# A state-space stage re-ordered by the size of the array pieces its matmuls use

## The chip, the cores and the metric

The kernel runs on one core of a Trainium2 chip, in one launch, all data in 32-bit floats. The metric is the device time of the launch in microseconds (us). Inside the core five engines run side by side, each with its own queue of instructions in a fixed order: TensorE (PE in the profile, its weight loads PEld), VectorE (DVE), ScalarE (ACT), GpSimd (POOL) and SyncE (SP), which issues most DMAs. TensorE writes only to PSUM; VectorE and ScalarE read the results from there.

## What is computed

Two layers on an image of 4 samples, 128 channels, 64 x 64 pixels. Layer 0 is three convolutions and an attention; layer 1 takes the pixels as 4 sequences of 4096 tokens through a state-space block run in both directions, and then through a recurrence. The change is in the state-space block:

```python
def _mamba3(x, in_proj, conv_w, conv_b, A_log, dt_bias, D, norm_w, out_proj):
    zxbcdt = x @ in_proj
    z, xbc, dt = jnp.split(zxbcdt, [D_INNER, D_INNER + CONV_DIM], axis=-1)
    xp = jnp.pad(xbc, ((0, 0), (K - 1, 0), (0, 0)))
    conv = sum((xp[:, i:i + l, :] * conv_w[:, i] for i in range(K))) + conv_b
    xh, Bm, Cm = jnp.split(_silu(conv), [D_INNER, D_INNER + D_STATE], axis=-1)
    dt = softplus(dt + dt_bias)
    A = -jnp.exp(A_log)
    y = _ssd(xh, dt, A, Bm, Cm) + xh * D[None, None, :, None]
    yg = y.reshape(b, l, D_INNER) * silu(z)
    yn = yg * rsqrt(jnp.mean(yg * yg, -1, keepdims=True) + EPS) * norm_w
    return yn @ out_proj

# _ssd, per chunk of tokens, per head (4 heads of 64 channels, 64 states):
Y_diag = einsum('bcln,bcsn,bchls,bcshp->bclhp', Cc, Bc, Lmat, xc)   # inside a chunk
states = einsum('bcln,bclh,bclhp->bchpn', Bc, decay_st, xc)         # what a chunk adds
new = st + carry * dec                                              # carried on
Y_off = einsum('bcln,bchpn,bclh->bclhp', Cc, prev, exp(Acs))        # from the carried state

t = t + _mamba3(ln(t), fwd...) + flip(_mamba3(flip(ln(t)), bwd...))
```


## The kernel before

The function `mamba` does both directions at once. Channels lie on the 128 partitions, tokens along the free axis. A **step** is a chunk of 128 tokens of each direction; a sequence has 32 steps and the four sequences follow one another, 128 steps in all. Four steps are a **group** of 512 tokens, 32 groups in all; j, from 0 to 3, is the place of a step in its group. Projections are made a group at a time, one group ahead.

The order on TensorE and ScalarE is that of the program text (`manual_schedule`, with these two engines); VectorE, GpSimd and SyncE get theirs from the scheduler of the framework. The loop over n (from line 1409 on) writes in each step:

- `states(m[n])`, L1212: what chunk n adds to the state, into `p_st`. Two matmuls with 64 output columns each, one for each direction: the two column halves of the array. VectorE adds it to the decayed state S (L1224).
- `turn(m[n+1])`, L1177: four 128 x 128 transposes of x of the next step into `ptr` (one buffer in PSUM). VectorE multiplies it by dt and by the decay into `xdt` and `xdtd` (L1196).
- `scan(m[n])`: eight matmuls `y<-lt,xdt` (L1234) in column halves, and then eight matmuls `y<-ct,S` (L1242) for the carried states, each with 64 rows and 64 columns, a quarter of the array.
- `prepare(m[n+1])`: the transpose of B into `p_bt` (L1187), two matmuls of B with C into `p_g` (L1189) with 64 rows and 128 columns each; then on ScalarE Exp of `lt` (L1191) and the copy `bt` (L1193); on VectorE xdt, xdtd, `gm` (L1200) and `lt` times gm (L1201); on GpSimd `ct` (L1202).
- `take`, for odd n: y plus D times x, on VectorE (L1254), which frees the PSUM tile y for the next two steps.
- projections by j. j = 0: px (L1124), pb for B (L1103), px. j = 1: pm, the means (L1283), px, pb for C. j = 2: px with four taps (L1115), four pz (L1146). j = 3: two po, the output (L1308).
- `differences(m[n+2])`: eight Relu on ScalarE (L1168) that prepare lt.
- on certain steps a part of a generator. `open_sequence(b+1)` prepares the next sequence: its first eight parts (steps 4 to 11 of a sequence) each transpose four tiles (`ls_in`, L83) for the row statistics, with bn_stats on VectorE (L85). `ended(b-1)` does the same for the sequence before, on odd steps from 5 on. For the last sequence `own` does it on steps 24, 25, 28 and 29.

All matmuls with px, pz and po use all 128 rows and 128 columns of the array (shown as `128*128`); pb uses column halves (`128*64`), the two directions being the halves. A 32-bit matmul runs as two rows in the profile, a transpose as one.

px, pb, pm, pz, po and ls_in take their PSUM from one pool, `ring`, with three buffers in turn: an allocation waits until the third one before it has been read out. Of px, ScalarE reads the first tap and VectorE three more (L1135, scalar_tensor_tensor), in place along x. `small` is one PSUM tile that holds `p_g`, `p_bt` and `p_st`.

Of the kernel before, what the change touches and what calls it, by code (L numbers as in the profile page):

```python
# [887 lines left out]
def mamba(nc, tc, k, a, t, B, T, vec, first=None, after=None, mr=None):  # L888
# [16 lines left out]
    with ExitStack() as ctx:  # L905
# [26 lines left out]
        bc_bias, dtb, A = vec["bc_bias"], vec["dtb"], vec["A"]  # L932
        wdt = wp.tile([P, QT], F32, name="wdt")
        nc.gpsimd.memset(wdt, 0.0)
        mean = wp.tile([P, QT], F32, name="mean")
        nc.gpsimd.memset(mean, 0.0)
        nc.gpsimd.memset(mean[:, 0:1], 1.0 / DI)
        with tc.tile_pool(name="m_ws", bufs=1) as ws, tc.tile_pool(name="m_wps", bufs=2, space=PSUM) as wps:
# [51 lines left out]
        ctx.enter_context(tc.manual_schedule(engines=set(engines)))  # L990
        small = ps.tile([P, 2, NC], F32, name="small")
        p_g, p_bt, p_st = small[:, :, 0:P], small[:, 0, P : 2 * P], small[:, 1, P : P + DI]

        def rows(g, i, c):

            return ds(g * MG + c if i == 0 else (NG - 1 - g) * MG + 2 * PAD - c, MG)
# [113 lines left out]
        def project_fwd(gr):  # L1110

            tl, g = gr["tl"], gr["at"][1]
            px = ring.tile([P, MG], F32, tag="big", name="px")
            for tap in range(KC):
                nc.tensor.matmul(px, w[0]["x"][:, tap, :], tl[:, rows(g, 0, tap)], start=(tap == 0), stop=(tap == KC - 1))  # L1115
            nc.scalar.activation(gr["x"][0][:, 0, :], px, AF.Silu, bias=w[0]["cb"][:, 0:1])

        def project(gr, i, c):


            tl, g = gr["tl"], gr["at"][1]
            px = ring.tile([P, MG], F32, tag="big", name="px")
            wx = w[1]["x"][:, bass.ts(c, P)] if i else w[0]["x1"]
            nc.tensor.matmul(px, wx, tl[:, rows(g, i, PAD)], start=True, stop=True)  # L1124
            x = gr["x+"][i][:, c, :]
            taps = w[i]["taps"][:, c, :]
            at = lambda n: x[:, PAD - n : PAD - n + MG] if i else x[:, n : n + MG]
            nc.vector.memset(x[:, 0:PAD] if i else x[:, MG:], 0.0)
            nc.scalar.activation(at(0), px, AF.Identity, scale=taps[:, PAD:KC], bias=w[i]["cb"][:, c : c + 1])  # L1129
            if g:  # L1130
                v = x[:, MG:] if i else x[:, 0:PAD]
                past = groups[gr["at"][0] * NG + g - 1]["x+"][i][:, c, :]
                nc.vector.tensor_tensor(v, v, past[:, 0:PAD] if i else past[:, MG:], ALU.add)
            for n in range(1, KC):
                nc.vector.scalar_tensor_tensor(at(n), px, taps[:, PAD - n : KC - n], at(n), ALU.mult, ALU.add)  # L1135
# [5 lines left out]
        def project_z(gr, i, c):  # L1141
            tl, g = gr["tl"], gr["at"][1]
            if c == 0:
                gr["z"][i] = grp.tile([P, 2, MG], F32, tag=f"z{i}", name=f"zT{i}", bufs=1)
            pz = ring.tile([P, MG], F32, tag="big", name="pz")
            nc.tensor.matmul(pz, w[i]["z"][:, bass.ts(c, P)], tl[:, rows(g, i, PAD)], start=True, stop=True)  # L1146
            nc.scalar.activation(gr["z"][i][:, c, :], pz, AF.Silu)

        def load(m):
# [20 lines left out]
        def turn(m):  # L1170

            gr, i = m["g"], m["i"]
            m["tok"] = [bass.ts(i % MT, P), bass.ts(MT - 1 - i % MT, P)]
            m["xh"] = ps.tile([P, ND, NHEAD, HD], F32, tag="tr", name="ptr")
            for d in range(ND):
                for c in range(2):
                    nc.tensor.transpose(  # L1177
                        m["xh"][:, d, 2 * c : 2 * c + 2, :].rearrange("p h c -> p (h c)"),
                        gr["x"][d][:, c, m["tok"][d]], k.ident,
                    )  # L1180

        def prepare(m):

            gr, i = m["g"], m["i"]
            Bs, Cs = gr["bc"][0], gr["bc"][1]
            cols = bass.ts(i % MT, P)
            nc.tensor.transpose(p_bt, Bs[:, cols], k.ident)  # L1187
            for d in range(ND):
                nc.tensor.matmul(p_g[:, d, :], Bs[HALF[d], cols], Cs[HALF[d], cols], start=True, stop=True)  # L1189
            lt = m["lt"]  # L1190
            nc.scalar.activation(lt, lt, AF.Exp, scale=-1.0)  # L1191
            m["bt"] = wk.tile([P, P], F32, tag="bt", name="bt")
            nc.scalar.copy(m["bt"], p_bt)  # L1193
            for name in ("dt", "dtd"):
                m[name] = wk.tile([P, ND, NHEAD, HD], F32, tag="x" + name, name="x" + name)
                nc.vector.tensor_tensor(  # L1196
                    m[name], m["xh"], m["b"][name][:, :, i, :].unsqueeze(3).to_broadcast([P, ND, NHEAD, HD]), ALU.mult
                )
            gm = wk.tile([P, ND, P], F32, tag="gm", name="gm")
            nc.vector.tensor_tensor(gm, p_g, k.tri, ALU.mult)  # L1200
            nc.vector.tensor_tensor(lt, lt, gm.unsqueeze(2).to_broadcast([P, ND, NHEAD, P]), ALU.mult)  # L1201
            nc.gpsimd.tensor_tensor(  # L1202
                m["ct"], m["ct"], Cs[:, cols].unsqueeze(1).to_broadcast([P, NHEAD, P]), ALU.mult
            )

        def states(m, S):
# [20 lines left out]
        def scan(m, y, S):  # L1227

            i = m["i"]
            at = [bass.ts(i % 2, P), bass.ts(1 - i % 2, P)]  # L1230
            for c in range(2):
                for d in range(ND):
                    for h in range(2):
                        nc.tensor.matmul(  # L1234
                            y[HALF[h], d, c, at[d]], m["dt"][:, d, 2 * c + h, :], m["lt"][:, d, 2 * c + h, :],
                            start=(i % 2 == 0 and c == 0), stop=(S is None), skip_group_check=True,
                        )
            if S is not None:
                for c in range(2):
                    for h in range(2):  # L1240
                        for d in range(ND):
                            nc.tensor.matmul(  # L1242
                                y[HALF[h], d, c, at[d]], S[HALF[d], 2 * c + h, :], m["ct"][HALF[d], 2 * c + h, :],
                                start=False, stop=True, skip_group_check=True,
                            )
# [13 lines left out]
        def half(d, i):  # L1259

            return bass.ts(i if d == 0 else 1 - i, 2 * P)
# [16 lines left out]
        def means(gr):  # L1278


            pm = ring.tile([ND * QT, MG], F32, tag="big", name="pm")
            for d in range(ND):
                nc.tensor.matmul(  # L1283
                    pm[bass.ts(d, QT)], mean, gr["z"][d][:, 0, :], start=True, stop=True, tile_position=(0, d * QT)
                )
            ms = wk.tile([ND * QT, MG], F32, tag="row", name="ms", bufs=3)
            nc.vector.tensor_scalar(ms, pm, RMS_EPS, None, ALU.add)
            n = ND * MG // P
            m1 = dram.tile([P, n], F32, tag="m1", name="m1")
            nc.sync.dma_start(m1.rearrange("(d q) n -> d (q n)", d=ND), ms[::QT])  # L1290
            col = wk.tile([P, n], F32, tag="col", name="col")
            nc.sync.dma_start(col, m1)
            rsqrt(nc, k, col, col)
# [10 lines left out]
        def outputs(gr, d):  # L1304
            po = ring.tile([P, MG], F32, tag="big", name="po")
            for i in range(2):
                for c in range(2):
                    nc.tensor.matmul(  # L1308
                        po[:, half(d, i)], w[d]["out"][:, c, :], gr["y"][d][i][:, c, :],
                        start=(c == 0), stop=(c == 1),  # L1310
                    )
            return po

        def means_here(gr):
# [88 lines left out]
        for i, c in STEPS_X:  # L1403
            activate(groups[0], i, c)
        turn(m[0])
        prepare(m[0])
        differences(m[1])
        S, y = None, None
        for n in range(N):
# [6 lines left out]
            if n % NT == 0:  # L1416
                S = None
            S1 = states(m[n], S)
            if n + 1 < N:
                turn(m[n + 1])  # L1420
            if n % 2 == 0:
                y = ps.tile([P, ND, 2, 2 * P], F32, tag="y", name="y")
            scan(m.pop(n), y, S)
            S = S1
            if n + 1 < N:
                prepare(m[n + 1])
            if n % 2:
                take(gr, j, y)
# [35 lines left out]
            if n + 2 < N:  # L1464
                differences(m[n + 2])

            i = n % NT
            if i == 4:
                opening = open_sequence(b + 1) if b + 1 < B else iter(())
            if i >= 4:  # L1470
                run(islice(opening, 1))
            if i == 5:
                ending = ended(b - 1) if after is not None and b > 0 else iter(())
            if i >= 5 and i % 2:
                run(islice(ending, 1))

            if mr is not None and b == B - 1 and i in (24, 25, 28, 29):
                if i == 24:
                    own = row_statistics(nc, k, ring, "big", wk, t[:, b * T :], mr, (3, 4, 2, 5, 1, 6))
                next(own)  # L1480
        squares(gr, (1,), True)
        if mr is not None:
            run(own)
# [273 lines left out]
```

## Time and profile before

| | |
|---|---|
| time, 3 runs | 3138.46, 3139.4, 3145.35 us; median 3139.4 |
| span of the profiled execution | 3147.0 us |
| state-space stage in it, first to last write of the states | 1718.7 to 2983.5 us |
| busy in that stretch (1264.8 us) | PE 1194.6, DVE 889.0, ACT 1014.1, POOL 725.0 us |
| mean granted TensorE clock in it | 0.98 |
| wait of PE at B's transpose for VectorE's S | 26 times, 26.4 us |

The profile is one execution. Its page has the busy time of each engine, the span in 40 slices, the chain of work that ended last, the costliest groups of instructions and the DMAs. Views of the trace answer for a stretch of time: the windows view gives the busy time of each engine in a stretch; the timeline gives instructions in order, each with start, duration, engine, line, operation, what it writes and reads, shape, count and, in brackets, the idle time before it and what ended it. Matmuls are pipelined and the end of each is modelled, so that neighbouring rows overlap: the step from one start to the next is what counts. The page puts the stage's lines low in its list because the attention before it has more instructions; the chain that ended last names PE first (26% of the span), with `pb L1103` as its costliest line (5%).

### The profile page before, as it was taken

What the parts mean: (1) busy time and instruction counts of PE and PEld (TensorE: products, weight loads), DVE (VectorE), ACT (ScalarE), POOL (GpSimd) and SP (SyncE); (2) the same over time, 40 slices, a digit from 0 to 9 for tenths busy, and PEclk for the clock granted to TensorE, in tenths of its full rate; (3) what the DMA queues carried; (4) which work ended last, traced back from release to release, by engine and by line L of the source; (5) the groups of instructions that cost most, each with busy time, mean ns of one, the idle gap of its engine ahead of it and who ended that gap; (6) DMA issues with size and microseconds to landing.
All of it is one profiled execution on the core that took longest, in us unless ns stands there. A gap on an engine that the chain in (4) does not pass through costs nothing. (4 is left out here: it accounts for less than half of the span.)

```text
span 3147.0 us, 42863 instructions
## 1 busy us (share of the span) xinstructions
PE 2925.4 (93%) x15511; PEld 1458.2 (46%) x15511; DVE 2195.2 (70%) x3429; ACT 1813.8 (58%) x3102; POOL 1798.5 (57%) x1393
## 2 busy tenths in 40 slices
PE   6799999999999999999997999999999999999976
PEld 1344444454444454444453444444444444455545
DVE  7876668666777667687765767776677766777667
ACT  3343434433444434444434878887788778888756
POOL 4258448456584665766553565565555565565644
PEclk9999999999999999999998999999999999999988
DMA  5310101010100101010023343334333343333332
GB/s 181 133 39 30 38 31 45 8 43 23 46 23 30 43 23 38 31 52 33 11 74 92 91 117 95 98 95 115 82 100 94 80 120 89 105 95 103 87 109 109
DMA packets 108394, 224.16 MB, mean 71 GB/s; under 512 B 25678, under 2 KB 29390, under 8 KB 106764
## 3 DMA queue, kind: packets, MB, share of 16 engines
q1 hardware_dynamic: 96588, 177.53, 19.9%
q10 hardware_dynamic: 11584, 43.78, 4.1%
q8 instruction: 125, 2.05, 0.3%
q14 instruction: 97, 0.79, 0.1%
HBM read 200.83 MB, written 20.44 MB: 70 GB/s over the span
## 5 line engine op out<-in xcount | busy, mean ns | idle before, releaser
L477 DVE TENSOR_TENSOR es<-es,ex 128x1024 f32<-128x1024 f32 x448 | 683.2, 1525 | 139.2 <-ACT ex L462 105.8
L462 ACT ACTIVATE ex<-pf 128x1024 f32<-128x1024 f32 x512 | 497.6, 1021 | 464.7 <-PE pf L460 421.2
L460 PE MATMUL pf<-theta,phi 64*128 64x512 f32 x2048 | 513.6, 619 | 20.4 <-ACT ex L462 20.0
L471 PE MATMUL acc<-ex,gT 128*64 128x512 f32 x2048 | 492.8, 607 | 1.7 <-ACT ex L462 1.7
L1202 POOL TENSOR_TENSOR ct<-ct,Cst 128x512 f32<-128x512 f32 x128 | 170.7, 1334 | 343.6 <-DMA ct<-csmem 314.1
L460 PEld LDWEIGHTS pf<-theta,phi 64*128 64x128 f32 x2048 | 173.0, 185 | 340.0 <-ACT ex L462 172.3
L1168 ACT ACTIVATE lt<-lt,cs 128x128 f32<-128x128 f32 x1024 | 312.1, 390 | 0.5 <-DMA lt<-csmem 0.5
L367 PE MATMUL pm<-yf,wt 128*128 128x256 f32 x1152 | 287.1, 382 | 11.9 <-DVE att L483 11.0
L410 ACT ACTIVATE eo<-pm 128x256 f32<-128x256 f32 x88 | 33.7, 383 | 448.9 <-PE pm L367 442.3
L471 PEld LDWEIGHTS acc<-ex,gT 128*64 128x64 f32 x2048 | 127.9, 137 | 339.8 <-issue 327.8
L367 PEld LDWEIGHTS pm<-yf,wt 128*128 128x128 f32 x1152 | 212.9, 189 | 93.4 <-issue 38.7
L1103 PE MATMUL pb<-tl,wbc_fwd 128*64 128x512 f32 x512 | 241.9, 616 | 6.5 <-DVE xT L1135 6.5
L1103 PE MATMUL pb<-tl,wbc_bwd 128*64 128x512 f32 x512 | 242.5, 617 | 0.0
L337 POOL TENSOR_TENSOR yf<-yd 128x272 f32<-128x272 f32 x192 | 234.0, 1246 | 1.4
L1267 POOL TENSOR_TENSOR yT<-yT,zT 128x512 f32<-128x512 f32 x127 | 166.5, 1316 | 58.1 <-DVE yT L1254 50.0
L337 POOL TENSOR_TENSOR yf<-xp 128x272 f32<-128x272 f32 x128 | 108.7, 880 | 136.0 <-PE pm L367 130.2
L1201 DVE TENSOR_TENSOR lt<-lt,gm 128x1024 f32<-128x1024 f32 x128 | 179.2, 1400 | 1.9
L1135 DVE SCALAR_TENSOR_TENSOR xT<-px,taps_bwd,xT 128x512 f32<-128x512 f32 x192 | 143.7, 748 | 8.7 <-ACT xT L1129 4.0
L1234 PE MATMUL y<-lt,xdt 128*64 128x128 f32 x2048 | 142.3, 282 | 7.6 <-PE ptr L1177 3.8
L1221 POOL TENSOR_TENSOR S<-S,tot 128x256 f32<-128x256 f32 x120 | 91.4, 762 | 100.7 <-PE y L1242 91.2
L1103 PEld LDWEIGHTS pb<-tl,wbc_fwd 128*64 128x64 f32 x512 | 66.9, 141 | 174.3 <-issue 142.9
L367 PE MATMUL pm<-yf,wc 128*128 128x256 f32 x512 | 131.3, 384 | 6.6 <-DVE att L483 5.1
(297 smaller groups left out, 5655.5 us busy)
## 6 DMA issues: line engine op xcount, KB each, us to landing
lt<-csmem SPq DMA_DIRECT2D x128, 512.0 KB, 5.7
wt<-wd ACTq DMA_DIRECT2D x72, 576.0 KB, 3.8
ct<-csmem SPq DMA_DIRECT2D x256, 128.0 KB, 5.2
rs<-m SPq DMA_DIRECT2D x31, 512.0 KB, 3.8
wd<-t SPq DMA_DIRECT2D x16, 576.0 KB, 2.8
t<-in_x SPq DMA_DIRECT2D x4, 2048.0 KB, 11.0
rows<-after SPq DMA_DIRECT2D x32, 256.0 KB, 4.4
out<-t SPq DMA_DIRECT2D x4, 2048.0 KB, 14.4
```

The costliest lines, as they stand in the source:

```text
L337: nc.gpsimd.tensor_tensor(f[:, kx], at(x), at(y), op)
L367: nc.tensor.matmul(pm[:, e, :], wt, src, start=(i == 0), stop=(i == len(terms) - 1))
L460: nc.tensor.matmul(pf[:, e, :], phi[HALF[e], m, :], th[HALF[e]], start=True, stop=True)
L462: nc.scalar.activation(ex, pf, AF.Exp, scale=scale)
L471: nc.tensor.matmul(acc[HALF[e]], gT[:, 2 * m + e, :], ex[:, e, :], start=(m == 0), stop=(m == NT // 2 - 1))
L477: nc.vector.tensor_tensor(es, es, ex, ALU.add)
L1103: nc.tensor.matmul(out, w[i]["bc"][:, tap, bass.ts(c, DS)], src, start=(tap == 0), stop=(tap == KC - 1),)
L1135: nc.vector.scalar_tensor_tensor(at(n), px, taps[:, PAD - n : KC - n], at(n), ALU.mult, ALU.add)
L1168: nc.scalar.activation(v, v, AF.Relu, scale=-1.0, bias=m["b"]["cs"][:, d, m["i"], h : h + 1])
L1201: nc.vector.tensor_tensor(lt, lt, gm.unsqueeze(2).to_broadcast([P, ND, NHEAD, P]), ALU.mult)
L1202: nc.gpsimd.tensor_tensor(m["ct"], m["ct"], Cs[:, cols].unsqueeze(1).to_broadcast([P, NHEAD, P]), ALU.mult)
L1267: eng.tensor_tensor(v, v, gr["z"][d][:, :, half(d, j // 2)], ALU.mult)
```

## The change

Five edits in `mamba`:

1. A new helper `product` makes a matmul with 128 output columns as two with 64 each, into partitions 0 to 63 and 64 to 127 of the result. px, pz and po use it. The means `pm` go to the two column halves too (the tile `mean` grows from 32 to 64 columns).
2. The carried states leave `scan` and become `carried`. A step now writes `states(n)`, `scan(n)`, `turn(n+1)`, then `carried(n)`.
3. The transpose of B of the next step moves from `prepare` to the end of `turn`.
4. B with C becomes `likeness`, right after `carried`: four matmuls with 64 rows and 64 columns in place of two with 64 and 128.
5. The first eight parts of `open_sequence`, all parts of `ended`, and `own` run between `turn` and `carried`, not at the end of the step. The later parts of `open_sequence` stay at the end.

```diff
-        mean = wp.tile([P, QT], F32, name="mean")
+        mean = wp.tile([P, HD], F32, name="mean")
...
+        def product(out, w, src, start=True, stop=True):
+            for half in HALF:
+                nc.tensor.matmul(out[half], w[:, half], src, start=start, stop=stop)
...
-                nc.tensor.matmul(px, w[0]["x"][:, tap, :], tl[:, rows(g, 0, tap)], start=(tap == 0), stop=(tap == KC - 1))
+                product(px, w[0]["x"][:, tap, :], tl[:, rows(g, 0, tap)], tap == 0, tap == KC - 1)
...
-            nc.tensor.matmul(px, wx, tl[:, rows(g, i, PAD)], start=True, stop=True)
+            product(px, wx, tl[:, rows(g, i, PAD)])
...
-            nc.tensor.matmul(pz, w[i]["z"][:, bass.ts(c, P)], tl[:, rows(g, i, PAD)], start=True, stop=True)
+            product(pz, w[i]["z"][:, bass.ts(c, P)], tl[:, rows(g, i, PAD)])
...
+            nc.tensor.transpose(p_bt, gr["bc"][0][:, bass.ts(i % MT, P)], k.ident)
+
+        def likeness(m):
+            Bs, Cs = (m["g"]["bc"][c] for c in range(2))
+            at = m["i"] % MT * P
+            for h in range(2):
+                for d in range(ND):
+                    nc.tensor.matmul(
+                        p_g[HALF[h], d, :], Bs[HALF[d], ds(at + h * DS, DS)], Cs[HALF[d], ds(at, P)],
+                        start=True, stop=True,
+                    )
 
         def prepare(m):
...
-            nc.tensor.transpose(p_bt, Bs[:, cols], k.ident)
-            for d in range(ND):
-                nc.tensor.matmul(p_g[:, d, :], Bs[HALF[d], cols], Cs[HALF[d], cols], start=True, stop=True)
...
+        def carried(m, y, S):
+            at = m["at"]
             if S is not None:
                 for c in range(2):
                     for h in range(2):
...
-            pm = ring.tile([ND * QT, MG], F32, tag="big", name="pm")
+            pm = ring.tile([P, MG], F32, tag="big", name="pm")
             for d in range(ND):
-                nc.tensor.matmul(
-                    pm[bass.ts(d, QT)], mean, gr["z"][d][:, 0, :], start=True, stop=True, tile_position=(0, d * QT)
-                )
-            ms = wk.tile([ND * QT, MG], F32, tag="row", name="ms", bufs=3)
+                nc.tensor.matmul(pm[HALF[d]], mean, gr["z"][d][:, 0, :], start=True, stop=True)
+            ms = wk.tile([P, MG], F32, tag="row", name="ms", bufs=3)
...
-                    nc.tensor.matmul(
-                        po[:, half(d, i)], w[d]["out"][:, c, :], gr["y"][d][i][:, c, :],
-                        start=(c == 0), stop=(c == 1),
-                    )
+                    product(po[:, half(d, i)], w[d]["out"][:, c, :], gr["y"][d][i][:, c, :], c == 0, c == 1)
...
             S1 = states(m[n], S)
+            if n % 2 == 0:
+                y = ps.tile([P, ND, 2, 2 * P], F32, tag="y", name="y")
+            scan(m[n], y, S)
+            at = n % NT
+            if at == 4:
+                opening = open_sequence(b + 1) if b + 1 < B else iter(())
+            if at == 5:
+                ending = ended(b - 1) if after is not None and b > 0 else iter(())
             if n + 1 < N:
                 turn(m[n + 1])
-            if n % 2 == 0:
-                y = ps.tile([P, ND, 2, 2 * P], F32, tag="y", name="y")
-            scan(m.pop(n), y, S)
+            turns = 4 <= at < 4 + NT // GT
+            if turns:
+                run(islice(opening, 1))
+            if at >= 5 and at % 2:
+                run(islice(ending, 1))
+            if mr is not None and b == B - 1 and at in (24, 25, 28, 29):
+                if at == 24:
+                    own = row_statistics(nc, k, ring, "big", wk, t[:, b * T :], mr, (3, 4, 2, 5, 1, 6))
+                next(own)
+            carried(m.pop(n), y, S)
             S = S1
             if n + 1 < N:
+                likeness(m[n + 1])
                 prepare(m[n + 1])
...
-            i = n % NT
-            if i == 4:
-                opening = open_sequence(b + 1) if b + 1 < B else iter(())
-            if i >= 4:
+            if at >= 4 and not turns:
                 run(islice(opening, 1))
-            if i == 5:
-                ending = ended(b - 1) if after is not None and b > 0 else iter(())
-            if i >= 5 and i % 2:
-                run(islice(ending, 1))
-
-            if mr is not None and b == B - 1 and i in (24, 25, 28, 29):
-                if i == 24:
-                    own = row_statistics(nc, k, ring, "big", wk, t[:, b * T :], mr, (3, 4, 2, 5, 1, 6))
-                next(own)
```

More of the change, by code (lines that the diff above doesn't have):

```diff
@@ L1180, in turn @@
                     )
+            nc.tensor.transpose(p_bt, gr["bc"][0][:, bass.ts(i % MT, P)], k.ident)
[8 more added lines that the diff above has]
+                    )
         def prepare(m):
             gr, i = m["g"], m["i"]
-            Bs, Cs = gr["bc"][0], gr["bc"][1]
             cols = bass.ts(i % MT, P)
-            nc.tensor.transpose(p_bt, Bs[:, cols], k.ident)
-            for d in range(ND):
-                nc.tensor.matmul(p_g[:, d, :], Bs[HALF[d], cols], Cs[HALF[d], cols], start=True, stop=True)
             lt = m["lt"]
@@ L1202, in prepare @@
             nc.gpsimd.tensor_tensor(
-                m["ct"], m["ct"], Cs[:, cols].unsqueeze(1).to_broadcast([P, NHEAD, P]), ALU.mult
+                m["ct"], m["ct"], gr["bc"][1][:, cols].unsqueeze(1).to_broadcast([P, NHEAD, P]), ALU.mult
             )
@@ L1229, in scan @@
             i = m["i"]
-            at = [bass.ts(i % 2, P), bass.ts(1 - i % 2, P)]
+            at = m["at"] = [bass.ts(i % 2, P), bass.ts(1 - i % 2, P)]
             for c in range(2):
@@ L1289, in means @@
             m1 = dram.tile([P, n], F32, tag="m1", name="m1")
-            nc.sync.dma_start(m1.rearrange("(d q) n -> d (q n)", d=ND), ms[::QT])
+            nc.sync.dma_start(m1.rearrange("(d q) n -> d (q n)", d=ND), ms[::HD])
             col = wk.tile([P, n], F32, tag="col", name="col")
@@ L1405, in mamba @@
         turn(m[0])
+        likeness(m[0])
         prepare(m[0])
```

## The prediction, made before the changed kernel ran

> **What bounds the kernel now.** I read the page's busy line first, then the state-space stage by windows, then one group of it engine by engine. A step is 128 tokens, a group four steps (j = 0 to 3); the stage has 32 groups. From the first write of the states (1718.7 us) to the last (2983.5) it takes 1264.8 us, 40% of the span. The page:
>
> ```profile
> PE 2925.4 (93%) x15511; PEld 1458.2 (46%) x15511; DVE 2195.2 (70%) x3429; ACT 1813.8 (58%) x3102; POOL 1798.5 (57%) x1393
> ```
>
> and one group, scan to scan, in the windows view (PE, PEld, DVE, ACT, POOL busy):
>
> ```profile
> 2774.08:2811.76 37.68, 37.38 (x264) 19.29 (x263) 27.46 (x65) 31.89 (x64) 23.01 (x20) 1.00 0.37 99
> ```
>
> TensorE hardly rests, at full clock. But ScalarE is at 85%, against 58% on the page: it is close behind. The TensorE timeline of that group:
>
> ```profile
> 2774.08 1.09 PE L1234 MATMUL y<-lt,xdt 128*64 128x128 f32 x16
> ...
> 2782.22 0.65 PE L1212 MATMUL small<-xdtd,bt 128*64 128x256 f32 x4
> 2782.80 0.66 PE L1177 MATMUL ptr<-ident,xT 128*128 128x128 f32 x4
> 2783.39 1.09 PE L1234 MATMUL y<-lt,xdt 128*64 128x128 f32 x16
> 2784.41 0.67 PE L1242 MATMUL y<-ct,S 64*64 64x128 f32 x16
> 2785.01 0.33 PE L1187 MATMUL small<-ident,Bst 128*128 128x128 f32 x1
> 2785.27 0.49 PE L1189 MATMUL small<-Cst,Bst 64*128 64x128 f32 x4
> 2785.69 1.05 PE L1283 MATMUL pm<-zT,mean 128*32 128x512 f32 x4
> 2786.68 1.13 PE L1124 MATMUL px<-tl,wx_bwd 128*128 128x512 f32 x2
> ...
> 2788.28 0.59 PE L1103 MATMUL pb<-tl,wbc_fwd 128*64 128x512 f32 x1
> 2788.29 0.59 PE L1103 MATMUL pb<-tl,wbc_bwd 128*64 128x512 f32 x1
> 2788.71 0.59 PE L1103 MATMUL pb<-tl,wbc_fwd 128*64 128x512 f32 x1
> ...
> 2791.39 0.66 PE L83 MATMUL ls_in<-ident,t 128*128 128x128 f32 x4
> ```
>
> The pair "128*64" is the piece of the array in use. A slot of a 512-wide row is 0.43 us (2788.28 to 2788.71), and two column halves share it. So a 128-wide slot is 0.107 and a 256-wide one 0.216. The scan has 16 rows in pairs, 8 slots = 0.86, but its start-to-start is 1.02: **0.16 us is the change of piece size**. The same rest stands at the transposes (4 slots 0.43 of 0.59), carried states (0.43 of 0.60), B's transpose (0.11 of 0.26) and likeness (0.21 of 0.42).
>
> **The change, TensorE alone.** Sizes now change 5 times inside each step, and around the projections 3+1 (j0), 3 (j1), 1+1 (j2), 1+1 (j3): 31 a group. Afterwards states, scan and projections share 128*64, all transposes 128*128, carried and likeness 64*64: 3 a step, 12 a group. 19 x 0.16 = 3.0 us. The full-array projections go too: eight px rows take 3.54 us here, 0.4425 each against 0.43 paired; 38 such rows, 0.5 us. Together 3.5 us a group, 112 us in 32.
>
> Two rules of the Trainium skill speak against this. "TensorE: Matmul & The Clock Gate", Part 3, says that a weight load overlaps a running matmul only where row groups differ. Column halves share their rows, so by the rule each of the 38 slots would pay a half-width load, 0.14 here: +5.3 us a group. The row decides: pb's next loads start at 2788.28 while its matmuls run, and the slot stays 0.43. I take nothing. Pairs here never share one moving operand as the new ones do; below, no gain over two turns (rival 4), above, 0.43; pb is nearest. "TensorEngine Tiling (Array Packing)", PSUM Bottleneck, warns that tiling speeds TensorE but not the emptying of its results. By slots alone I would write 112 us; the rows below side with the warning.
>
> **j0 and j1: VectorE takes it back.** Times from the first scan (2774.08 = 0). Before, the second scan starts at 9.31. After: scan and change 1.02, five transposes and change 0.70, carried, likeness and change 0.82, px 0.91, pb 3.44, px 0.86, states 0.43 = 8.18. Gained: 1.13. But the next turn now stands behind this scan, not before it. It ends at 8.18+1.02+0.43 = 9.63 (before 8.72+0.43 = 9.15), and the first product with x reads it. VectorE executes in order:
>
> ```profile
> 2783.50 0.69 DVE L1196 TENSOR_TENSOR xdt<-ptr,dt 128x512 f32<-128x512 f32 x1
> 2784.89 0.75 DVE L1135 SCALAR_TENSOR_TENSOR xT<-px,taps_fwd,xT 128x512 f32<-128x512 f32 x1
> 2787.00 0.74 DVE L1135 SCALAR_TENSOR_TENSOR xT<-px,taps_fwd,xT 128x512 f32<-128x512 f32 x1
> ```
>
> The built order of the changed kernel keeps xdt before the three tap products of j0's last px. Those empty its PSUM slot; the pool has three, and the third allocation after it is pb of j1 (px of j1 where an ls_in lies between). xdt is at 9.63+0.27 = 9.90 (before 9.42), then xdt 0.60, taps 0.67, xdtd 0.60, taps 0.66, y 0.39, taps 0.74: free at 13.56. pb starts at 13.6 (before 13.66) and ends at 17.04 (before 17.14). **Of 1.6 us, 0.1 is left.** With an ls_in, bn_stats (0.21 each) replace xdtd and y: free at 12.99, px and pb end at 17.33, where before pb ended at 17.31 and ls_in's 0.59 followed.
>
> **j2 and j3: ScalarE takes it back.** From pb's end to the next group's scan ScalarE runs without a pause; its row marks the last slack:
>
> ```profile
> 2791.50 0.69 ACT L1107 ACTIVATE Cst<-pb,bc_bias 128x512 f32<-128x512 f32 x1 [1.55 <-PE pb L1103]
> ...
> 2799.19 0.69 ACT L1116 ACTIVATE xT<-px,cb_fwd 128x512 f32<-128x512 f32 x1 [0.85 <-PE px L1115]
> ```
>
> Start to start: to Cst 0.27, Cst 0.59, eight differences 2.45, table 1.29, Exp 0.96, bt 0.27, table 1.28, four x 2.14, four z with the ring's wait 2.29, differences 2.46, table 1.30, Exp 0.96, bt to gm 0.28; then VectorE gm 0.34, y 0.39, lt 1.16, y to the scan that reuses its PSUM 0.57: **19.0 us**. TensorE's path was 19.3 without ls_in and falls to about 17.2, so the chain decides: 0.3 gained. Group without ls_in: 36.44 before (37.68 less 0.59, 0.54 and a 0.12 wait), 17.04+19.0 = 36.04 after: **0.4**. With two: the built order puts rs (0.61) between gm and lt, 19.6; 17.33+19.6 = 36.9 against 37.68: **0.7**. With four (39.68 at 1795.0): ls_in in j0 adds 0.43; 37.4: **2.3**.
>
> Groups: the opening of a sequence puts ls_in in steps 4 to 11, two groups in each of three sequences, 6 x 2.3 = 13.8; 8 with two, 5.6; 12 with none, 4.8. In the other 6 (steps 16-19 and 24-27 of the first three sequences, openings waiting for POOL and VectorE; 44.4 and 42.2 us in the first sequence) TensorE waits for their chain anyway: 0. **Sum 24 us.**
>
> Small edits: mean to 64 columns leaves pm at two slots (0.98 now, 0.91 after); its VectorE reading doubles partitions, not length, same 0.68. B's transpose before carried adds a wait: for VectorE's S. Behind it on TensorE stand carried and likeness, and ScalarE's bt waits with them. Before, it waited 26 times, 26.4 us. S now stands ahead of bn_stats: 0, at worst 0.3 a group. ls_in moved before carried has the same three slots, in the same cyclic order; the moved closing part takes its row copy and SP's store along, once a sequence, under 1 us. SP's loads of lt and ct keep their place; ct is ready (2792.45) long before its use (2805.2).
>
> The profiled execution's span, 3147.0, lies 7.6 (0.24%) above the median. Off the span 24 leaves 3123; **off the median 3115 us**.
>
> **Rivals.** (1) TensorE's sum holds: 3139-112 = 3027, or up to 3095 where the chains give half. For it: TensorE waits little now. Against: ScalarE's 31.9 of 37.68. 0.16. (2) No change: the 0.4 and 0.7 vanish in jitter and the openings too. 0.17. (3) Slower: the moved turn holds VectorE's queue longer in j1. lt takes 1.92 in this group when POOL is busy, 1.22 otherwise; if xdt to the last tap grows by 0.9, pb ends 0.8 later than before, a group loses 0.4, 32 x 0.4 = 13: 3152. It decides from 0.4 us more than I count. 0.14. (4) The halves of one product take turns: 22 slots of 0.43 and 16 of 0.216, 12.9 us less the slack of 1.5, 11.4 x 32 = 365: 3504. All pairs of the trace speak against it. 0.03. The forecast: 0.50.
>
> **Numbers.** The range takes the forecast, half of rival 1 and most of 2 and 3: 3070 to 3150; the likeliest case alone 3095 to 3133. 0.2% is 6.3 us, about what a measurement of this kernel can tell from no change. Faster 0.50+0.16 = 0.66, same 0.17, slower 0.14+0.03 = 0.17.
>
> **What would show it.** Right: the halves of px within 0.02 us; second scan about 8.2 after the first in a j0 without ls_in; pb (or px) of j1 waiting 1 us for VectorE's taps; scan after j3 waiting 1 to 2 us for lt or y; ScalarE over 87% of a group; TensorE busy down. Wrong: groups under 34 us (the chains are not tight), or pairs of 0.86 us.

## The result, and the profile after

The changed kernel takes 3116.15 us (median of 4 runs, 3112.35 to 3119.64), the kernel before 3139.65 in the same session (4 runs, 3138.46 to 3145.35). The ratio is 0.992, with a 95% interval from 0.9905 to 0.9934: 23.5 us faster. The profiled execution took 3119.64, its span is 3117.8. In the stage, from the start of the first scan to that of the last (these are the 1718.7 and 2983.5 us of the table above), the two profiles differ by 1264.8 - 1240.9 = 23.9 us; their spans by 29.2, of which 5.3 lie outside this stretch.

The page's busy line shows where TensorE stands (busy time, share of the span, instructions):

```profile
PE 2835.3 (91%) x17239; PEld 1427.6 (46%) x17239; DVE 2210.2 (71%) x3429; ACT 1815.4 (58%) x3102; POOL 1800.0 (58%) x1393
```

TensorE works 90 us less than before (2925.4), and the kernel gains a quarter of that. The windows view of the group that the prediction worked on (span of the window, length, then busy time of PE, PEld, DVE, ACT, POOL, the clock and the DMAs) says the same for 37 us:

```profile
2745.37:2782.34 36.97, 34.05 (x316) 18.39 (x317) 28.07 (x65) 31.98 (x64) 22.04 (x20) 1.00 0.38 101
```

TensorE's busy time falls by 3.3 us, the group only by 0.7. The rest is now waiting, as TensorE's timeline of this group shows (start, duration, operation, and in brackets the idle time before it with what ended it):

```profile
2753.54 1.05 PE L1247 MATMUL y<-lt,xdt 128*64 128x128 f32 x16
2754.52 0.66 PE L1182 MATMUL ptr<-ident,xT 128*128 128x128 f32 x4
...
2758.42 1.08 PE L997 MATMUL px<-tl,wx_bwd 128*64 128x512 f32 x4 [0.87 <-DVE xT L1140]
...
2772.62 1.08 PE L997 MATMUL pz<-tl,wz_bwd 128*64 128x512 f32 x4 [0.70 <-ACT zT L1152]
...
2782.34 1.09 PE L1247 MATMUL y<-lt,xdt 128*64 128x128 f32 x16 [1.35 <-issue]
```

The second scan starts 8.17 us after the first, but px of j1 then waits for VectorE's taps, and the scan after j3 waits for the PSUM tile y. For the last wait the profile names no releaser ("issue"); that it is y is read from VectorE's rows, the last tap and the last reading of y:

```profile
2757.55 0.73 DVE L1140 SCALAR_TENSOR_TENSOR xT<-px,taps_fwd,xT 128x512 f32<-128x512 f32 x1
...
2781.39 0.86 DVE L1271 SCALAR_TENSOR_TENSOR yT<-xT,D_bwd,y 128x256 f32<-128x256 f32 x2
```

They end at 2758.28 and 2782.25; px starts at 2758.42 and the scan at 2782.34. Over the whole kernel, the waits view of after (total, times, longest) has

```profile
PE y L1247 <- issue: 42.0, 26, 2.8
PE small L1186 <- DVE S L1237: 19.8, 12, 3.8
...
PE px L997 <- DVE xT L1140: 10.7, 11, 1.4
```

where the one of before had

```profile
PE small L1187 <- DVE S L1224: 26.4, 26, 4.2
...
PE y L1234 <- issue: 2.5, 2, 1.4
```

In the stage TensorE is busy 86 us less and idle 62 us more (132.2, before 70.2). The wait for y, which went from 2.5 to 42.0 us, is the largest part of that. By place in the group, and over the 31 groups measured from scan to scan, j0 gains 40.8 us and j2 13.4; j1 loses 3.2, and j3, with the wait for y, 22.9.

The scan-to-scan times of these groups by class, from one trace of each kernel. *Open* are the six groups with four ls_in, *ls* the four of the last sequence with two, *first* the first of each sequence, *blocked* the six costed at nothing; steps 44 and 76 start the groups behind the openings of the second and third sequence. *Ls* and the *other 9* are called the quiet groups below. Sums in us:

| kernel | first | open | blocked | 44 and 76 | ls | other 9 | all 31 |
|---|---|---|---|---|---|---|---|
| before | 146.8 | 249.0 | 267.1 | 86.6 | 150.6 | 343.8 | 1243.9 |
| after | 154.8 | 236.2 | 263.8 | 76.3 | 147.9 | 336.8 | 1215.9 |
| pairs alone | 145.4 | 246.7 | 266.9 | 82.6 | 148.4 | 337.4 | 1227.4 |
| after, whole array | 149.2 | 238.7 | 264.6 | 78.0 | 151.3 | 343.2 | 1225.1 |
| after, turn ahead | 146.3 | 248.6 | 268.0 | 81.6 | 150.7 | 341.3 | 1236.5 |
| after, parts at the end | 152.5 | 253.5 | 263.2 | 86.2 | 158.0 | 337.6 | 1250.9 |
| after, B's transpose behind | 147.4 | 240.3 | 262.9 | 77.9 | 150.1 | 343.1 | 1221.8 |
| after, differences of j2 | 149.4 | 235.7 | 254.6 | 73.2 | 144.6 | 337.9 | 1195.4 |

These 31 groups gain 28.0 us. The last one, which has no next group to project, takes 24.9 us from its first scan to its last, before 20.9: it loses 4.0.

### The profile page after: what moved, and what is told of

It is laid out like the page before. It is cut to its first block, busy times and chain, and to the rows that moved or that the text cites. A ratio compares the mean times of both kernels' runs of the same rounds, so it can differ in the third digit from the quotient of the medians.

```text
span 3117.8 us, 46442 instructions
## 1 busy us (share of the span) xinstructions
PE 2835.3 (91%) x17239; PEld 1427.6 (46%) x17239; DVE 2210.2 (71%) x3429; ACT 1815.4 (58%) x3102; POOL 1800.0 (58%) x1393
## 5 line engine op out<-in xcount | busy, mean ns | idle before, releaser
L460 PE MATMUL pf<-theta,phi 64*128 64x512 f32 x2048 | 513.8, 619 | 20.5 <-ACT ex L462 20.1
L1215 POOL TENSOR_TENSOR ct<-ct,Cst 128x512 f32<-128x512 f32 x128 | 183.4, 1433 | 231.7 <-DMA ct<-csmem 210.6
L1108 PE MATMUL pb<-tl,wbc_fwd 128*64 128x512 f32 x512 | 232.4, 597 | 11.9 <-DVE xT L1140 11.9
L1108 PE MATMUL pb<-tl,wbc_bwd 128*64 128x512 f32 x512 | 233.4, 598 | 0.0
L1284 POOL TENSOR_TENSOR yT<-yT,zT 128x512 f32<-128x512 f32 x127 | 167.6, 1329 | 23.2 <-DVE yT L1271 19.9
L1234 POOL TENSOR_TENSOR S<-S,tot 128x256 f32<-128x256 f32 x120 | 86.9, 724 | 159.2 <-PE y L1259 154.8
L1247 PEld LDWEIGHTS y<-lt,xdt 128*64 128x64 f32 x2048 | 124.9, 141 | 80.1 <-issue 56.5
L1209 DVE TENSOR_TENSOR xdt<-ptr,dt 128x512 f32<-128x512 f32 x128 | 88.2, 689 | 91.0 <-PE ptr L1182 90.9
L1140 DVE SCALAR_TENSOR_TENSOR xT<-px,taps_bwd,xT 128x512 f32<-128x512 f32 x192 | 143.7, 748 | 12.1 <-ACT xT L1134 4.6
```

The lines of the kernel that those rows point to most:

```text
L460: nc.tensor.matmul(pf[:, e, :], phi[HALF[e], m, :], th[HALF[e]], start=True, stop=True)
L1108: nc.tensor.matmul(out, w[i]["bc"][:, tap, bass.ts(c, DS)], src, start=(tap == 0), stop=(tap == KC - 1),)
L1247: nc.tensor.matmul(y[HALF[h], d, c, at[d]], m["dt"][:, d, 2 * c + h, :], m["lt"][:, d, 2 * c + h, :], start=(i % 2 == 0 and c == 0), stop= ...
L1284: eng.tensor_tensor(v, v, gr["z"][d][:, :, half(d, j // 2)], ALU.mult)
```

## Experiments

Theory A is the prediction's: VectorE's queue in j0 and j1 and ScalarE's in j2 and j3 take back most of what TensorE saves. All ratios below are to the kernel before, timed beside each run.

**1. The two halves of the change apart.** First the changed kernel with px, pz and po on the whole array (the order, the likeness and the means as in after):

```diff
         def product(out, w, src, start=True, stop=True):
-            for half in HALF:
-                nc.tensor.matmul(out[half], w[:, half], src, start=start, stop=stop)
+            nc.tensor.matmul(out, w, src, start=start, stop=stop)
```

> The changed kernel, with px, pz and po on the whole array again (product makes one matmul of 128 columns). Theory A (VectorE's queue between px of j0 and pb of j1, and ScalarE's chain from pb to the next group's scan, set the period; TensorE's time is mostly cover): only j0 and the start of j1 are on the path there, some 3 changes of piece size and 4 rows, 0.5 us a group in about 26 groups: +13 us, 3129. Theory B (TensorE's sum sets the time): 8 more changes of 0.16 and 38 rows of 0.0125 a group, 1.8 us x 32 = +56 us, 3172.

Measured: 3127.0 us, ratio 0.9967 (0.9956 to 0.9978): theory A's number. Then the kernel before with nothing but `product` for px, pz and po:

```diff
-            nc.tensor.matmul(px, wx, tl[:, rows(g, i, PAD)], start=True, stop=True)
+            product(px, wx, tl[:, rows(g, i, PAD)])
...
-            nc.tensor.matmul(pz, w[i]["z"][:, bass.ts(c, P)], tl[:, rows(g, i, PAD)], start=True, stop=True)
+            product(pz, w[i]["z"][:, bass.ts(c, P)], tl[:, rows(g, i, PAD)])
```

> The kernel before, with px, pz and po as pairs of column halves and nothing else. Theory A: j0's px ends 0.4 us earlier and pb of j1 follows it, ScalarE's chain gives 0.3 more and then holds: 0.7 us a group, -22 us, 3117: about what the whole change brings. Theory B: 1.8 us a group, -56 us, 3083.

Measured: 3130.64 us, ratio 0.9975 (0.9964 to 0.9987), 14 us above theory A's number and further from B's. The order (with the likeness and the means) is worth 12.1 us, the pairs 8.5, together 20.6 of the 23.5: the two nearly add, and neither comes near TensorE's slot count. In no class are the pairs slower, as halves that take turns would be. By classes they do different things: the pairs give the gain of the quiet groups (*ls* 148.4, after 147.9), the order most of that of *open* and of 44 and 76.

**2. Where B's wait for the state hits: the turn and the parts ahead of the states.**

```diff
-            S1 = states(m[n], S)
...
-            scan(m[n], y, S)
             at = n % NT
...
                 next(own)
+            S1 = states(m[n], S)
...
+            scan(m[n], y, S)
             carried(m.pop(n), y, S)
```

> The changed kernel, with the transposes (turn and the parts of the openings) ahead of states, so that a step is transposes, states, scan, carried. TensorE changes piece size 4 times a step, not 3. Theory A: xdt can start some 1.3 us earlier, pb of j1 stops waiting for the taps of px, and the turn of j3 fills the wait ahead of the next scan: pb of j1 ends 1.5 us earlier, 1.5 x 32 = -48 us, 3068 (3060 to 3085). Theory B: one more change a step, 4 x 0.16 x 32 = +20 us, 3136.

Measured: 3138.12 us, ratio 0.9998 (0.9988 to 1.0008). The gain that I put on the early turn isn't there; the number is theory B's, but the waits changed as well (y 5.2 us in place of 42.0, S 47.1 in place of 19.8), so it doesn't speak for B's sum. TensorE's timeline and VectorE's of this kernel, in j1 of a group with two ls_in:

```profile
2765.82 0.45 PE L1194 MATMUL small<-Cst,Bst 64*64 64x128 f32 x8 [1.83 <-DVE S L1237]
```

```profile
2761.39 0.69 DVE L1209 TENSOR_TENSOR xdt<-ptr,dt 128x512 f32<-128x512 f32 x1 [0.23 <-PE ptr L1182]
...
2763.07 0.73 DVE L1140 SCALAR_TENSOR_TENSOR xT<-px,taps_fwd,xT 128x512 f32<-128x512 f32 x1
...
2764.66 0.71 DVE L1140 SCALAR_TENSOR_TENSOR xT<-px,taps_fwd,xT 128x512 f32<-128x512 f32 x1
...
2765.36 0.41 DVE L1237 TENSOR_TENSOR S<-S,small 128x256 f32<-128x256 f32 x1
```

xdt is early, as meant, and the last tap ends 11.8 us after the group's first scan, in after 12.9. But bn_stats and taps now stand ahead of the state's sum S. The likeness, which writes the same PSUM tile `small`, waits for S: 47.1 us in 41 waits over the kernel. So xdt's place does hold up the taps, and freeing them gained nothing here, since the next row of the same queue held TensorE in their stead. The run doesn't separate this from its other effects: the states are written later, and there is one more change of piece size a step.

**3. The tap wait taken away:** pb ahead of px in j1.

```diff
                 if more:
-                    project(groups[G + 1], *STEPS_X[2])
-                if more:
                     project_bc(groups[G + 1], 1)
+                if more:
+                    project(groups[G + 1], *STEPS_X[2])
```

> The changed kernel, with pb before px in j1; the same instructions. Theory A: pb (3.4 us) runs while VectorE still reads j0's last px, and px takes the slot that is waited for; C is ready some 1.4 us earlier, and after px ScalarE's differences start 0.75 us earlier: 0.75 us a group, -20 us, 3096. Theory B: TensorE has the same work, 3116; rival C (the wait of 0.9 us on px or pb is only a symptom, VectorE's total delay comes back at the next step): 3116 too.

Measured: 3111.87 us, ratio 0.9919 (0.9902 to 0.9935), not told apart from after, as theory B and rival C had it. px of the group shown before no longer waits, yet the group takes 37.08 us. ScalarE's timeline of this kernel, and of after, at the same place:

```profile
2762.04 0.69 ACT L1112 ACTIVATE Cst<-pb,bc_bias 128x512 f32<-128x512 f32 x1 [1.87 <-PE pb L1108]
2762.90 0.78 ACT L1134 ACTIVATE xT<-px,cb_bwd,taps_bwd 128x512 f32<-128x512 f32 x1 [0.17 <-PE px L997]
2763.58 2.43 ACT L1173 ACTIVATE lt<-lt,cs 128x128 f32<-128x128 f32 x8
```

```profile
2762.99 0.69 ACT L1112 ACTIVATE Cst<-pb,bc_bias 128x512 f32<-128x512 f32 x1 [1.36 <-PE pb L1108]
2763.57 2.43 ACT L1173 ACTIVATE lt<-lt,cs 128x128 f32<-128x128 f32 x8
```

Cst is 0.95 us earlier, ScalarE's first tap of px (the `Identity` of the expectations, L1134) has moved into the room, and the differences start at the same time. So a wait of 0.9 us on TensorE was worth nothing while ScalarE's chain follows.

**4. ScalarE's chain shortened:** the differences of j1 and j2 on VectorE.

```diff
+                    if here:
+                        nc.vector.tensor_scalar(
+                            v, v, m["b"]["cs"][:, d, m["i"], h : h + 1], 0.0, ALU.subtract, ALU.min
+                        )
+                        continue
...
-            nc.scalar.activation(lt, lt, AF.Exp, scale=-1.0)
+            nc.scalar.activation(lt, lt, AF.Exp, scale=m["sign"])
...
-                differences(m[n + 2])
+                differences(m[n + 2], j in (1, 2))
```

> The changed kernel, with the differences of two of the four steps of a group (16 rows of 0.30 us) computed by VectorE instead of ScalarE. Theory A, the one of the prediction: from the end of B's and C's projection in j1 to the next group's scan ScalarE's queue is the bound (19.35 us from the start of C's activation to the scan, while TensorE has some 17.3 us of work there). It loses 4.9 us, so TensorE's own 17.3 us decide: up to 1.8 us a group in 28 groups, 50 us, 3066 us; the wait of the first scan on the activated z and the wait for the rescaled likeness go. Rival B: VectorE's queue is as long there; its 16 added rows of about 0.2 us push the taps, the state's sum and the rescale back by what ScalarE gives up: 3116 us, or up to 3130.

Measured: 3233.77 us, ratio 1.0292 (1.0275 to 1.0309): theory A missed by 168 us, the rival by 104. With the edit of experiment 3 as well:

> Both edits: in j1 the projection of B and C ahead of that of x, and the differences of two steps on VectorE. Theory A: with ScalarE relieved, C's activation no longer stands behind the Identity of px and the wait on the taps is out of the way, so the gains add: 3055 to 3062 us. Rival: the same time as with the differences alone, within 4 us, since either the tap wait or ScalarE's queue is off the path.

Measured: 3227.7 us, ratio 1.0278 (1.0254 to 1.0301); 6 us less than without, which says little beside such a loss. VectorE's timeline of the first of these two kernels has the cause:

```profile
2836.25 6.20 DVE L1175 TENSOR_SCALAR lt<-lt,cs 128x128 f32<-128x128 f32 x6 [1.72 <-DMA lt<-csmem]
...
2859.86 1.46 DVE L1175 TENSOR_SCALAR lt<-lt,cs 128x128 f32<-128x128 f32 x7
```

Seven such rows take 1.46 us in j2; six take 6.20 at the end of j0, where the scheduler put those of j1, ahead of px's taps. The taps, S and B's transpose then come late: TensorE waits 5.79 us there, 156.3 in all. But from Cst (2853.79) to the next group's scan (2871.54) this kernel needs 17.75 us, in place of 19.35: this points to ScalarE's chain, under a loss elsewhere. So the differences of j2 alone, for which VectorE has idle time:

```diff
-                differences(m[n + 2], j in (1, 2))
+                differences(m[n + 2], j in (2,))
```

> The changed kernel, with the differences of j2 alone (8 rows a group) on VectorE, where it stands idle 4 us for the state's matmul. Theory A, ScalarE's chain: the run with two sets moved had 17.5 us from C's activation to the next group's scan in place of 19.3, although it lost more than that in j1; this one has nothing added to j1 and gives 1.4 to 1.8 us in 26 to 28 groups, 36 to 50 us: 3066 to 3080 us. Rival B, VectorE's queue is the bound wherever rows are added to it: 3116 us or more.

Measured: 3102.45 us, ratio 0.9889 (0.9861 to 0.9916): 14 us faster than after, between the two expectations. The same group's window:

```profile
2726.93:2762.76 35.83, 34.07 (x316) 18.42 (x317) 28.20 (x73) 29.77 (x55) 22.40 (x19) 1.00 0.41 104
```

The group is 1.14 us shorter with TensorE's work unchanged and ScalarE's 2.2 us less: ScalarE's chain did bound it. The waits view of this kernel tells why the whole gained 14 us and not 36:

```profile
PE small L1192 <- DVE S L1243: 43.2, 22, 5.7
...
PE y L1253 <- issue: 8.6, 6, 2.1
```

The wait for y fell from 42.0 to 8.6 us, and the wait for S rose from 19.8 to 43.2; the last three steps of the stage take 29.9 us, in after 24.9. With pb first besides:

> The same with B's and C's projection ahead of that of x in j1. Theory A: the tap wait (0.87 us in the groups with parts) is out of TensorE's path, and as ScalarE no longer decides, it counts now: up to 0.9 us more in some 24 groups, 3050 to 3062 us. Rival: ScalarE still takes px's Identity behind C's activation (0.78 us) and decides: the same time as the differences of j2 alone, within 4 us.

Measured: 3102.89 us, ratio 0.9882 (0.9865 to 0.9898): the rival. The tap wait stays worthless.

**5. The place of B's transpose:** behind the carried states again.

```diff
         def turn(m):
...
-            nc.tensor.transpose(p_bt, gr["bc"][0][:, bass.ts(i % MT, P)], k.ident)
...
         def likeness(m):
...
             at = m["i"] % MT * P
+            nc.tensor.transpose(p_bt, Bs[:, ds(at, P)], k.ident)
```

> The changed kernel, with B's transpose put back behind the carried states, directly ahead of the likeness. Theory A: the wait of that transpose for VectorE's state sum (19.8 us in all, 12 times, most in the first groups of the sequences, which lost 0.6 to 3.3 us each) is a cost of the change that the prediction had at nothing: the wait is covered by the carried states' 0.5 us and part of it goes, 6 to 10 us, 3108 us. Rival: the transpose only shows a delay that starts at the transfer of ct and the clock; the same delay then ends at the likeness or the scan, and the time stays at 3116 us within 3.

Measured: 3123.0 us, ratio 0.994 (0.9924 to 0.9957). That is some 7 us slower than after, which neither expected; the intervals overlap a little, the runs don't. The table shows both signs: *first* gets back 7.4 of the 8.0 us lost, *open* loses 4.1, *ls* 2.2 and the *other 9* 6.3. A 128 x 128 transpose between two 64 x 64 stages is two more changes of piece size: j0 of a quiet group takes 8.5 us, in after 8.2. So only where it waited, in j1 and in step 16 of a sequence:

```diff
-                turn(m[n + 1])
+                turn(m[n + 1], not (j == 1 or at == 16))
...
             if n + 1 < N:
+                if j == 1 or at == 16:
+                    turn_b(m[n + 1])
                 likeness(m[n + 1])
```

> The changed kernel, with B's transpose behind the carried states in j1 and in step 16 of a sequence only: the steps in which it waited for the state's sum. With it behind the carried states everywhere, three of the first groups of the sequences gained 0.9 to 4.4 us, but j0 and j3 of nearly every group lost 0.2 to 0.3 us. Theory A: the wait of B's transpose is a real cost of the change and the loss is the two more changes of piece size in steps where nothing covers them; here the gains stay and the losses go: 6 to 12 us, 3107 us. Rival: the wait only moves to the rows behind it (VectorE's x times dt stands behind the state's sum as well): 3116 us within 3.

Measured: 3114.1 us, ratio 0.9933 (0.9916 to 0.9949): the rival. The S wait falls to 14.1 us, *first* to 150.6, and the median hardly moves. With the differences of j2 on VectorE:

> The same with the differences of j2 on VectorE, where B's transpose waited 43 us for the state's sum. Theory A: the two gains add, and of the larger wait some 12 us go: 3088 to 3096 us. Rival: 3102 us within 3.

Measured: 3100.5 us, ratio 0.9878 (0.9862 to 0.9895). It is the fastest of all, not told apart from the one without B's late transpose.

**6. The moved parts:** openings, endings and closing statistics at the end of the step again, all else as after.

```diff
-            turns = 4 <= at < 4 + NT // GT
-            if turns:
-                run(islice(opening, 1))
-            if at >= 5 and at % 2:
-                run(islice(ending, 1))
...
             carried(m.pop(n), y, S)
...
-            if at >= 4 and not turns:
+            if at >= 4:
                 run(islice(opening, 1))
+            if at >= 5 and at % 2:
+                run(islice(ending, 1))
```

> The changed kernel, with the parts of openings, endings and closing statistics back at the end of a step. Theory A: their projection ahead of those of B, C and x is what made the gain of the groups with such parts (2.0 and 2.3 us in the opening groups and 0.7 us in those with two, as against 0.4 without): 6 x 1.9 + 8 x 0.3 us, 14 us, are given back, 3130 us. Rival: the gain comes from the turn alone and the place of these parts is worth nothing: 3116 us within 3.

Measured: 3150.49 us, ratio 1.0037 (1.0016 to 1.0057), slower than before, and 20 us above what I expected. Its timelines, TensorE and then VectorE, of j1 in a group with two ls_in:

```profile
2793.12 0.33 PE L1186 MATMUL small<-ident,Bst 128*128 128x128 f32 x1 [1.51 <-DVE S L1237]
```

```profile
2791.34 0.74 DVE L1140 SCALAR_TENSOR_TENSOR xT<-px,taps_bwd,xT 128x512 f32<-128x512 f32 x1
2791.99 0.49 DVE L85 BATCH_NORM_STATS2 ls_st<-ls_in 128x6 f32<-128x128 f32 x2
2792.40 0.37 DVE L87 BATCH_NORM_AGGREGATE mr<-ls_st 128x2 f32<-128x6 f32 x4
2792.67 0.39 DVE L1237 TENSOR_TENSOR S<-S,small 128x256 f32<-128x256 f32 x1
```

With ls_in ahead of the states, its statistics and the taps stand ahead of S, and B's transpose waits (51.9 us in 40 waits). Where B's transpose moves, the parts have to move with it: the change without the parts is 34 us slower than with them.

## Why the prediction was right, and where not

**The size, 24 us: right in sum, and that by luck in part.** Measured 23.5. The rates of the prediction (2.3, 0.7, 0.4 and 0 us a group) give each class a share, which the traces answer so (gains in us):

| class | predicted | measured |
|---|---|---|
| first (4 groups) | 1.6 | -8.0 |
| open (6) | 13.8 | 12.8 |
| blocked (6) | 0 | 3.3 |
| 44 and 76 (2) | 1.4 | 10.3 |
| ls (4) | 2.8 | 2.7 |
| other 9 | 3.9 | 7.0 |
| the last one | 0.7 | -4.0 |

*Open* and *ls*, for which the working was done row by row, came out. The rest missed by 15 us upwards and by 14 us downwards, and the two cancel.

**TensorE alone, 112 us: right in a quiet group, three quarters of it in the stage.** In the group it is busy 3.3 us less where I had 3.5. A change of piece size costs what the rows said: the second scan is at 8.17 where the sum gave 8.18. In the stage it is busy 1194.6 us before and 1108.7 after, 86 less. Part of the rest is the clock: in the last three steps TensorE is busy 19.9 us at a mean clock of 0.73, before 15.7 at 1.00.

**Two halves in one slot: right.** px's four rows take 1.08 us, and the pairs alone make the kernel faster. No load was added to the slot.

**j0 and j1 give all but 0.1 back: right in size, read from the rows and not isolated.** px starts at 13.05 where the sum had its slot free at 12.99, and pb's slots end at 17.37, where it had 17.33. That xdt's place holds up the taps agrees with experiment 2, where they end 1.1 us sooner. What I had not seen is that S, in the same queue, then holds TensorE instead.

**ScalarE in j2 and j3: right, and shown** by experiments 3 and 4. The chain measures 19.6 us from pb's end, my number. Groups with two ls_in gain 0.67 us each in *ls* (predicted 0.7), the opening groups 12.8 (predicted 13.8). ScalarE is busy 31.98 of 36.97 us, 86.5%; I had asked for over 87.

**The step that failed is "B's transpose before carried adds a wait: for VectorE's S ... 0, at worst 0.3 a group."** It was wrong in both directions. In the first groups of the second and third sequence S is late, and TensorE waits 1.82 and 3.06 us for it. The chain in the third, on GpSimd, ScalarE and TensorE, one after the other:

```profile
2343.13 2.35 POOL L1215 TENSOR_TENSOR ct<-ct,Cst 128x512 f32<-128x512 f32 x1 [5.52 <-DMA ct<-csmem]
```

```profile
2352.67 0.63 ACT L1290 ACTIVATE zT<-yT 128x512 f32<-128x512 f32 x1 [3.54 <-POOL yT L1284]
```

```profile
2357.27 0.47 PE L1186 MATMUL small<-ident,Bst 128*128 128x128 f32 x1 [3.06 <-DVE S L1237]
```

GpSimd waits for the load of ct, ScalarE's square (zT) for GpSimd, its first tap of px stands behind the square, VectorE's taps and S behind that. I had written that ct is ready long before its use, from a group in the middle of a sequence; the opening of a sequence was not looked at. The same chain was there before, and ended in a wait of 0.81 us, where B's transpose stood behind the carried states:

```profile
2378.21 0.33 PE L1187 MATMUL small<-ident,Bst 128*128 128x128 f32 x1 [0.81 <-DVE S L1224]
```

Not all of the 8.0 us lies at this wait. Over the four first groups j1 loses 5.4 us and j3, where TensorE waits for y, 4.6; j0 and j2 gain 2.0. Experiment 5 gets 7.4 back by moving the transpose, but in experiment 3, which leaves it in place, the four groups take 150.4 us in place of 154.8. So the place of the transpose costs time there; how much of the 8.0 us is its doing is not firm.

In the other direction, the S waits of before held a gain that I counted at nothing. At steps 44 and 76 two parts at the end of one step had put two sets of statistics ahead of S:

```profile
2159.58 0.33 PE L1187 MATMUL small<-ident,Bst 128*128 128x128 f32 x1 [2.02 <-DVE S L1224]
```

Behind this wait TensorE ran 4.40 us at a mean clock of 0.63. The two groups gain 10.3 us together; at the rate of a group with two ls_in, 0.7 each, they would have had 1.4. With the parts at the end of the step (experiment 6) they take 86.2 us, before 86.6.

**The last group, 4.0 us lost, was not in the sum.** The turn, which now stands behind a scan that no projection follows, isn't the cause by itself: experiment 6 has it in the same place and takes 20.1 us there, after 24.9 and before 20.9. What differs between those two kernels is the place of the moved parts, here those that close the last sequence (`own`). In after they wait for t from GpSimd, ahead of the carried states, and the clock in these steps is 0.73, in experiment 6 0.92:

```profile
2936.52 1.11 PE L83 MATMUL ls_in<-ident,t 128*128 128x128 f32 x4 [1.13 <-POOL t L1361]
```

How the loss divides between this wait, those around it and the clock stays open.

**Rivals.** TensorE's sum (3027 to 3095) is out, though the 3095 doesn't follow from its sum, half of the 112 us being 3083: after takes 3116, and the run with ScalarE relieved in j2 still 3102. "No change" is out by the interval, which ends at 0.9934. "Slower" had the right place, VectorE's queue in j1, and decides in the two slow kernels of experiment 4.

## What to carry to other kernels

When a step of the order is moved, list for each waiting instruction what the other engine's queue has ahead of the row it waits for, in the openings and first groups as well as in a quiet one. A wait on one engine is worth its length only if the next engine's chain doesn't refill it: test by removing the wait, and then by shortening the chain. And count a re-ordering whole: this one, with its moved parts left at the end of the step, was slower than the kernel before.

## What the runs showed of the hardware

**VectorE beside GpSimd.** In the first kernel of experiment 4 the difference (128x128, one tensor operand) takes VectorE 0.27 to 0.30 us in the 246 rows beside which GpSimd does nothing, and up to 1.37 when GpSimd works. Six took 6.20 us from 2836.25 to 2842.45, and GpSimd's rows there end at 2842.36:

```profile
2838.65 2.49 POOL L1299 TENSOR_TENSOR zT<-zT 128x512 f32<-128x512 f32 x2
2841.10 1.26 POOL L1221 TENSOR_TENSOR ct<-ct,Cst 128x512 f32<-128x512 f32 x1
```

About one difference went through per GpSimd row of 1.25 us, which agrees with what the Trainium skill's "SBUF — State Buffer", section "Who interferes with whom", states as a lock: a tensor_scalar, which the difference is, can enter a mode that takes a pair of ports shared with GpSimd, and then the later of the two waits for the whole instruction of the other. That this mode was in use is not shown by any trace here. Where GpSimd rests, in j2 of the kernel with those of j2 alone, eight of them took 1.65 us.

**A wait costs more than its length.** In the first group of the third sequence TensorE's clock fell behind the 3.06 us wait (windows before, around and behind it; the clock is the third number from the right):

```profile
2344.83:2354.20 9.37, 9.37 (x77) 4.94 (x77) 4.76 (x10) 4.16 (x8) 9.37 (x8) 1.00 0.24 57
2354.20:2357.20 3.00, 0.01 (x1) 0.00 (x0) 2.82 (x6) 2.99 (x6) 2.69 (x3) 0.91 0.44 137
2357.20:2362.00 4.80, 4.73 (x33) 2.33 (x35) 4.80 (x12) 4.27 (x10) 0.61 (x1) 0.50 0.38 82
2362.00:2370.00 8.00, 8.00 (x71) 3.84 (x71) 6.53 (x11) 5.32 (x12) 1.88 (x3) 0.91 0.07 23
```

At a clock of 0.50 for 4.8 us, about 2.4 us more are lost than the wait itself (an estimate, 4.8 times 0.50). The waits of 0.87 and 1.35 us in the quiet group above left the clock at 1.00.
